# A selective-scan kernel: in the blocks behind a projection, the side chain runs one place later

## The chip, the cores and the metric

One core of a Trainium2 chip runs the whole program. The metric is the device time of one execution in microseconds (us), as the median of several runs. Smaller is better.

## The reference, cut to what matters

Sixteen images of 64 x 64 pixels and 96 channels go through two layers, each added to its input. Layer 0 normalises, upsamples with a Fourier interpolation, applies two 1 x 1 projections with a quadratic between them, and downsamples again. Layer 1 normalises, projects, convolves 3 x 3, and then runs a selective scan in four directions over the 4096 pixels. The scan is what fills the time:

```
delta = softplus(dts + dt_bias)
h = exp(dt * A) * h + (dt * u) * b
y = sum over the 16 states of h * c
```

`dts`, `b` and `c` are projections of the convolved rows `u`; there are 192 channels, 16 states and four directions. At the end the four results are added, normalised, gated and projected back to 96 channels.

## The kernel before, in words

**The scan.** The function `scan` (line 831) goes over 128 *steps*: each of the 16 images has 8, namely 4 forward and then 4 backward, and a step covers 1024 pixels. A step has six *blocks* (line 826), and a block four *units*. One unit (lines 1165 to 1249) covers two groups, "odd" and "even", of 128 partitions each:

- `decay` (L1039) is an exponential on ScalarE (ACT) into PSUM, one for each of the two groups. There is one PSUM buffer for each group, so the next decay waits until VectorE (DVE) is done with the last one.
- `drive` (L1045) is a product of 128 x 2048 on GpSimd (POOL). It is issued two units ahead.
- `recur` (L1054 forward, L1056 backward) is the scan itself, on DVE, first the odd group, then the even one.
- The read-out multiplies by `c`: on DVE for the even group (L1225); for the odd group on POOL (L1208) in units 0 to 2, and on DVE (L1215) in unit 3. `read_out` (L1079) then sums over the states with 16 small matmuls on TensorE (PE), eight a group.
- `keep` (L1062) copies the last state of a group, which the next step starts from.

**Places.** Every unit has three places, called with `slot(0)`, `slot(1)` and `slot(2)` (L1202, L1224, L1231): after the odd scan, after the even scan, and at the end behind the even read-out product, the next even decay and `read_out`. At each of them one step is taken of `all_work` (L916), the side chain, and after it perhaps one of the background (L1141). So a block has twelve places, p = 0 to 11; place p is place p mod 3 of unit p // 3. Every engine executes its own queue in the order in which the instructions were issued here.

**The side chain.** For each block one `task` (L878) makes 512 columns of `delta` (the softplus) and of the *step-size product* `dtu` that the next step needs. It starts with a matmul for `s` (L886), then ACT takes the *magnitude* m and e = exp(-m) (L893, L894), then w = 1 + e and the *logarithm* d (L897, L898), then ACT finishes w (L901) and PE adds *four sums* into `s` (L903), then DVE makes `dtu` from `s` (L907), ACT copies `delta` (L908), and both go to DRAM (L910, L911). In blocks 2 and 3 of a step the projection `pp` of the next step (L866) is issued at the last place, p = 11, and it uses the same PSUM buffer as `s`. So in the blocks behind a projection, blocks 3 and 4, the task is *late*: first ACT must empty `pp` with the copy `pr` (`mixed`, L871; its two writes of `rows` to DRAM go to a list that SyncE (SP) empties with the next units), and only then `s` may start. The late task has shorter pauses (the `late` counts at L891, L895, L899). Before the change these places are: copy 1, `s` 2, magnitude 4, logarithm 5, four sums 7, `dtu` 10, writes 11.

**The background.** While an image is scanned, `front` (L301) prepares the next one and `finish` (L591) ends the last one, a small piece at a time, mostly at the third place of a unit. In the fourth image's scan, steps 0 to 3 hold the quadratic layer, steps 4 and 5 the convolution (L556, with its two ACT_TABLE_LOADs around the Silu at L572 to L574), and the end of step 5 to step 7 the normalisation and output of the image before (L620 to L672). In `finish`, `rooted` (L641) makes a DVE product (L642) of the matmul `o_ps` (L697).

Of the kernel before, what the change touches and what calls it, by code (L numbers as in the profile page):

```python
# [78 lines left out]
def tile_two_blocks(  # L79
# [141 lines left out]
    def send(kept=0):  # L221
        while len(put_off) > kept:
            args, kwargs = put_off.pop(0)
            nc.sync.dma_start(*args, **kwargs)
# [606 lines left out]
    def scan():  # L831


        with ExitStack() as es:
# [13 lines left out]
            def open_step(st):  # L848
                ctxs[st].update(
                    rows=dctx.tile([2, 2 * NS, T], F32, name="rows"),  # L850
                    delta=[dctx.tile([128, T], F32, name=f"delta_d{v}") for v in range(3)],
                    dtu=[dctx.tile([128, T], F32, name=f"dtu_d{v}") for v in range(3)],
                    pr={},
                )

            def fetch_u(st, v, t):
                mi, _, lc = steps[st]
                uv = up_.tile([128, TB], F32, name="u")
                nc.sync.dma_start(out=uv, in_=image[mi]["xs"][v, :, lc * T + t:lc * T + t + TB])
                return uv  # L860

            def mix(st, us, ps):
                pair = steps[st][1]
                pp = ps.tile([128, TB], F32, name="pp", tag="g")
                for v in range(3):
                    nc.tensor.matmul(pp, lhsT=xpt_s[:, pair, v, :], rhs=us[v], start=(v == 0), stop=(v == 2))  # L866
                return pp

            def mixed(st, t, pp):
                pr = prp.tile([128, TB], F32, name="pr")  # L870
                nc.scalar.activation(pr, pp, AF.Identity, bias=bumps_s)  # L871
                for r in range(2):
                    later(
                        out=ctxs[st]["rows"][r, :, t:t + TB], in_=pr[64 * r:64 * r + 2 * NS, :]
                    )
                ctxs[st]["pr"][t] = pr

            def task(st, k, ps, make, late=False):  # L878

                v, t = tasks[k]
                ctx, pair = ctxs[st], steps[st][1]
                u = fetch_u(st, v, t)
                s = ps.tile([128, TB], F32, name="s", tag="g")
                nc.tensor.matmul(  # L886
                    s, lhsT=dtw_s[:, pair, v, :], rhs=ctx["pr"][t], start=True, stop=False, skip_group_check=True
                )
                yield
                e, d, m, w = (make(k) for k in ("e", "d", "m", "w"))  # L890
                for _ in range(1 if late else 2):  # L891
                    yield
                nc.scalar.activation(m, s, AF.Abs, scale=2.0)  # L893
                nc.scalar.activation(e, m, AF.Exp, scale=-1.0)  # L894
                for _ in range(1 if late else 2):  # L895
                    yield
                nc.scalar.activation(w, e, AF.Identity, bias=one_s)  # L897
                nc.scalar.activation(d, e, AF.Ln, bias=one_s)  # L898
                for _ in range(2 if late else 3):  # L899
                    yield  # L900
                nc.scalar.activation(w, w, AF.Identity, scale=-1.0, bias=one_s)  # L901
                for by, of in ((half_s, m), (ident_s, w), (ident_s, e), (ident_s, d)):
                    nc.tensor.matmul(s, lhsT=by, rhs=of, start=False, stop=(of is d), skip_group_check=True)  # L903
                for _ in range(3):
                    yield
                dtu, delta = make("dtu"), make("delta")
                nc.vector.tensor_mul(dtu, s, u)  # L907
                nc.scalar.copy(delta, s)  # L908
                yield
                nc.sync.dma_start(out=ctx["dtu"][v][:, t:t + TB], in_=dtu)  # L910
                nc.sync.dma_start(out=ctx["delta"][v][:, t:t + TB], in_=delta)  # L911
# [4 lines left out]
            def all_work(mi_of):  # L916

                chain = [(st + (k > 5), k % 6) for st in range(len(steps)) for k in (3, 4, 5, 6, 7, 8)]
                current = task(*chain[0], gps, near)
                next(current)  # L920
                pp = waiting = None
                for b in range(len(chain)):
                    mine, bi = divmod(b, len(blocks))
                    more = mine + 1 < len(steps)
                    for p in range(3 * NQ):
                        if pp is not None and p == 1:
                            mixed(*pp)
                            pp = None
                        elif p == 2 and waiting is not None:
                            current, waiting = waiting, None  # L930
                        if current is not None:
                            next(current, None)
                        if more and bi in (2, 3):
                            if p == 3:
                                if bi == 2:
                                    if steps[mine + 1][0] > mi_of():
                                        ahead_gen.drain()
                                        send()
                                    open_step(mine + 1)
                                us = [fetch_u(mine + 1, v, TB * (bi - 2)) for v in range(3)]  # L940
                            elif p == 11:
                                pp = mine + 1, TB * (bi - 2), mix(mine + 1, us, gps)
                        if p == 11:
                            current = None
                            if b + 1 < len(chain) and chain[b + 1][0] < len(steps):
                                if pp is not None:
                                    waiting = task(*chain[b + 1], gps, near, True)
                                else:
                                    current = task(*chain[b + 1], gps, near)
                                    next(current)  # L950
                        yield
# [195 lines left out]

            last = len(units) - 1
            work = all_work(lambda: mi)
            for n in range(2):  # L1150
                drive(n)
# [13 lines left out]
            for n, (st, bi, j) in enumerate(units):  # L1165
# [71 lines left out]
                if j == 1 and n + 3 <= last and steps[units[n + 3][0]][1] == 1:  # L1237
                    st2, bi2, _ = units[n + 3]
# [124 lines left out]
```

## Time and profile before

| what | value |
|---|---|
| median of 3 runs | 20050.83 us (20045.97 to 20051.76) |
| the profiled execution | 20052.4 us |
| its span, first to last instruction | 20050.6 us |
| granted TensorE clock, mean | 0.876 |
| ACT busy | 13339.3 us (67%) |
| PE busy | 16526.3 us (82%) |
| DVE waits for ACT `da`, L1056 and L1054 | 135.8 + 99.7 + 30.7 + 7.4 us |
| ACT waits for PE before the copy `pr` L871 | 251.1 us, 134 times |
| ACT waits for PE before the magnitude L893 | 223.6 us, 124 times |
| DVE waits for PE before `dtu` L907 | 198.4 us, 57 times (the longest, 149.9 us, before the scan starts) |

An engine that is busy for most of the span need not be the bound at a given place: idle time counts where the engine that sets the pace stands still. The profile names, for each idle stretch, what released the engine. A line of the timeline reads: start, duration, engine, source line, operation, result <- inputs, shape, count, and in brackets the idle time before it.

### The profile page before, as it was taken

Reading aid. Unit: us, or ns where it says so; the run is one execution under the profiler, and the core shown is the slowest. Engines: PE = TensorE matmul, PEld = TensorE weight load, DVE = VectorE, ACT = ScalarE, POOL = GpSimd, SP = SyncE. Lnnn points to the kernel's source line nnn. Section 1 sums busy time; section 2 is a strip of 40 time slices with the busy share of each in tenths; the row PEclk is TensorE's granted clock in tenths of the full one; section 3 lists DMA queues with packets and bytes.
Section 4 is the critical chain, followed back from the end, with each engine's and each line's share of the span. In section 5 each row is a group of like instructions: output and inputs, shape, how many; then the busy total and the mean of one; then the engine's idle time right before and its main releaser. Section 6 shows DMA issues by size and latency. Waiting matters only on the chain. (4 is left out here: it accounts for less than half of the span.)

```text
span 20050.6 us, 275225 instructions
## 1 busy us (share of the span) xinstructions
PE 16526.3 (82%) x98604; PEld 7189.9 (36%) x98604; DVE 19133.1 (95%) x13040; ACT 13339.3 (67%) x19798; POOL 19176.4 (96%) x5403
## 2 busy tenths in 40 slices
PE   7877888888888888888888888888888888887965
PEld 4423334333343433334333343333434334343321
DVE  1999999999999999999999999999999999999999
ACT  4666766667666676767667666676666766666654
POOL 1999999999999999999999999999999999999999
PEclk8887898988889888898988889889898888989977
DMA  3666676766667666676766767667676676767755
GB/s 90 218 232 208 231 236 217 242 220 231 231 221 239 218 231 235 221 243 215 235 229 222 242 211 242 221 223 242 212 249 213 231 237 218 246 209 238 247 209 186
DMA packets 1979481, 4481.77 MB, mean 224 GB/s; under 512 B 465022, under 2 KB 564254, under 8 KB 1976190
## 3 DMA queue, kind: packets, MB, share of 16 engines
q1 hardware_dynamic: 1978110, 4464.15, 65.4%
q8 instruction: 779, 12.76, 0.3%
q14 instruction: 592, 4.85, 0.1%
HBM read 3585.05 MB, written 878.18 MB: 223 GB/s over the span
## 5 line engine op out<-in xcount | busy, mean ns | idle before, releaser
L1045 POOL TENSOR_TENSOR b<-dtu,bt 128x2048 f32<-128x2048 f32 x3072 | 13913.0, 4541 | 527.6 <-DMA dtu<-dtu_d 464.4
L1039 ACT ACTIVATE da<-delta,a_s 128x1024 f32<-128x1024 f32 x6144 | 6850.4, 1115 | 2264.7 <-DVE b L1225 799.1
L1208 POOL TENSOR_TENSOR odd<-b,ct 128x1024 f32<-128x1024 f32 x2304 | 5445.3, 2363 | 296.1 <-DVE b L1056 196.2
L1079 PE MATMUL y<-b,fold_s 128*32 128x256 f32 x30720 | 2642.5, 439 | 2559.4 <-DVE b L1225 2534.7
L1225 DVE TENSOR_TENSOR b<-da,ct 128x1024 f32<-128x1024 f32 x3072 | 3748.3, 1220 | 13.6
L1056 DVE TENSOR_TENSOR_SCAN da<-da,new,b 128x1024 f32<-128x1024 f32 x1440 | 3337.8, 2336 | 113.0 <-ACT da L1039 100.2
L1054 DVE TENSOR_TENSOR_SCAN da<-da,new,b 128x1024 f32<-128x1024 f32 x1440 | 3339.1, 2337 | 31.6 <-ACT da L1039 16.2
L1062 ACT COPY new<-da 128x1 f32<-128x1 f32 x2880 | 453.4, 157 | 3345.1 <-DVE b L1225 1842.5
L1079 PEld LDWEIGHTS y<-b,fold_s 128*32 128x32 f32 x30720 | 744.1, 116 | 4729.1 <-DVE b L1225 2708.6
L1056 DVE TENSOR_TENSOR_SCAN b<-da,new,b 128x1024 f32<-128x1024 f32 x864 | 2020.9, 2339 | 52.0 <-ACT da L1039 51.6
L1054 DVE TENSOR_TENSOR_SCAN b<-da,new,b 128x1024 f32<-128x1024 f32 x864 | 2022.5, 2341 | 0.1
L1079 PE MATMUL y<-odd,fold_s 128*32 128x256 f32 x18432 | 1609.6, 423 | 121.5 <-POOL odd L1208 116.1
L556 PE MATMUL c_ps<-xgp,wtap_s 96*64 96x512 f32 (+1 forms) x4608 | 1645.2, 609 | 5.5 <-ACT xgp L523 5.5
L422 PE MATMUL h_ps<-wide,w1t_s 96*128 96x500 f32 x1920 | 1114.6, 693 | 178.7 <-ACT wide L429 102.0
L449 PE MATMUL o_ps<-w2c_s,wide 128*100 128x96 f32 x9600 | 1071.8, 277 | 87.5 <-ACT wide L429 85.6
L449 PEld LDWEIGHTS o_ps<-w2c_s,wide 128*100 128x100 f32 x9600 | 1031.4, 191 | 277.9 <-ACT wide L429 155.8
L1056 DVE TENSOR_TENSOR_SCAN da<-da,b 128x1024 f32<-128x1024 f32 x480 | 1085.5, 2280 | 41.1 <-ACT da L1039 35.6
L1054 DVE TENSOR_TENSOR_SCAN da<-da,b 128x1024 f32<-128x1024 f32 x480 | 1084.0, 2277 | 39.1 <-POOL b L1045 24.7
L903 PE MATMUL s<-m,half_s 128*128 128x512 f32 x1534 | 1071.3, 787 | 1.0 <-ACT m L893 1.0
L886 PE MATMUL s<-pr,dtw_s 128*128 128x512 f32 x1536 | 1068.1, 784 | 0.0
L903 PE MATMUL s<-w,ident_s 128*128 128x512 f32 x1534 | 947.6, 704 | 141.8 <-ACT w L901 139.3
L556 PEld LDWEIGHTS c_ps<-xgp,wtap_s 96*64 96x64 f32 (+1 forms) x4608 | 593.1, 168 | 939.1 <-issue 904.7
(179 smaller groups left out, 21896.6 us busy)
## 6 DMA issues: line engine op xcount, KB each, us to landing
dtu<-dtu_d SPq DMA_DIRECT2D x1536, 512.0 KB
delta<-delta_d SPq DMA_DIRECT2D x1536, 512.0 KB
bt<-rows SPq DMA_DIRECT2D x1024, 512.0 KB
ct<-rows SPq DMA_DIRECT2D x1024, 512.0 KB
u<-xs_d SPq DMA_DIRECT2D x1544, 256.0 KB
dtu_d<-dtu SPq DMA_DIRECT2D x767, 256.0 KB
delta_d<-delta SPq DMA_DIRECT2D x767, 256.0 KB
wide<-in_x SPq DMA_DIRECT2D x768, 128.0 KB
```

The source lines that it names most:

```text
L422: nc.tensor.matmul(h_ps[j], lhsT=w1t_s[:, 128 * j:128 * (j + 1)], rhs=xu.rearrange("c p q -> c (p q)"), start=True, stop=True,)
L449: nc.tensor.matmul(o_ps[:, p, :], lhsT=hsq[j][:, UPS * p:UPS * (p + 1)], rhs=w2c_s[:, j, :], start=(j == 0), stop=(j == HB - 1),)
L556: nc.tensor.matmul(c_ps[p:p + n], lhsT=wtap_s[:, tap, 128 * i:128 * i + n], rhs=xgp[:, h0:h0 + 8, dx:dx + HW], start=(tap == 0), stop=(tap ...
L886: nc.tensor.matmul(s, lhsT=dtw_s[:, pair, v, :], rhs=ctx["pr"][t], start=True, stop=False, skip_group_check=True)
L903: nc.tensor.matmul(s, lhsT=by, rhs=of, start=False, stop=(of is d), skip_group_check=True)
L1039: nc.scalar.activation(da, deltas[n // NQ, e], AF.Exp, scale=a_s[:, k, g, units[n][2]:units[n][2] + 1])
L1045: nc.gpsimd.tensor_mul(b, dtus[n // NQ], bt.unsqueeze(1).to_broadcast([128, 2, T]))
L1054: nc.vector.tensor_tensor_scan(out, da, b, before, ALU.mult, ALU.add)
L1056: nc.vector.tensor_tensor_scan(out[:, ::-1], da[:, ::-1], b[:, ::-1], before, ALU.mult, ALU.add)
L1079: nc.tensor.matmul(y[32 * q:32 * q + 32, e, :], lhsT=fold_s, rhs=weighed[e][:, QT * q:QT * q + QT], start=(pair == 0 and j == 0 and e == 0 ...
L1208: nc.gpsimd.tensor_mul(odds[n], h, bc[1, r, j])
L1225: nc.vector.tensor_mul(bs[n][:, 0, :], h, bc[1, r, j])
```

## The change

`late` tasks get everything up to the four sums one place later, and one pause less between the sums and `dtu`. The late places become: copy 2, `s` 3, magnitude 5, logarithm 6, four sums 8, `dtu` 10, writes 11. Blocks that are not behind a projection, and the order on DVE and POOL, stay as they were. The `rows` writes of a late copy are handed to SP one unit later.

```
@@ task
                 for by, of in ((half_s, m), (ident_s, w), (ident_s, e), (ident_s, d)):
                     nc.tensor.matmul(s, lhsT=by, rhs=of, start=False, stop=(of is d), skip_group_check=True)
-                for _ in range(3):
+                for _ in range(2 if late else 3):
                     yield
                 dtu, delta = make("dtu"), make("delta")
@@ all_work
                     for p in range(3 * NQ):
-                        if pp is not None and p == 1:
+                        if pp is not None and p == 2:
                             mixed(*pp)
                             pp = None
-                        elif p == 2 and waiting is not None:
+                        elif p == 3 and waiting is not None:
                             current, waiting = waiting, None
```

More of the change, by code (lines that the diff above doesn't have):

```diff
@@ L903, in task @@
                     nc.tensor.matmul(s, lhsT=by, rhs=of, start=False, stop=(of is d), skip_group_check=True)
-                for _ in range(3):
+                for _ in range(2 if late else 3):
                     yield
@@ L925, in all_work @@
                     for p in range(3 * NQ):
-                        if pp is not None and p == 1:
+                        if pp is not None and p == 2:
                             mixed(*pp)
                             pp = None
-                        elif p == 2 and waiting is not None:
+                        elif p == 3 and waiting is not None:
                             current, waiting = waiting, None
```

## The prediction

> **What bounds the kernel.** I read the page's first part, then the stages of one image (the fourth) as windows, then what POOL and DVE waited for, then the timeline of single blocks.
>
> ```profile
> PE 16526.3 (82%) x98604; PEld 7189.9 (36%) x98604; DVE 19133.1 (95%) x13040; ACT 13339.3 (67%) x19798; POOL 19176.4 (96%) x5403
> ```
>
> Two engines look full. The windows (length, then busy time of PE, PEld, DVE, ACT, POOL) tell them apart; these are steps 2, 4, 5 and 6:
>
> ```profile
> 4393.94:4542.80 148.86, 132.00 (x1121) 74.70 (x1122) 148.07 (x103) 104.04 (x165) 148.86 (x43) 0.83 0.65 223
> 4691.91:4843.76 151.85, 119.10 (x668) 42.59 (x668) 145.98 (x108) 115.19 (x180) 149.40 (x43) 0.90 0.68 236
> 4843.76:4995.07 151.31, 126.67 (x588) 50.41 (x588) 148.47 (x103) 110.79 (x153) 150.82 (x43) 0.92 0.72 242
> 4995.07:5156.35 161.28, 137.94 (x600) 48.49 (x600) 152.71 (x112) 100.20 (x146) 150.88 (x43) 0.91 0.77 257
> ```
>
> In step 2 POOL never rests: 148.86 us is POOL's own work, 24.8 us a block. A step costs more only where POOL waits: about 3 us more in steps 4 and 5, 12 in step 6 (and 11 in step 7, 2.6 in step 1). So a DVE stall costs only what it makes POOL wait.
>
> How much DVE may be late follows from POOL's queue. The last unit of a block has no odd product, so behind the product for a block's first unit POOL has a whole further product (4.55) before the odd one that needs DVE's odd scan (2.34). DVE may start a block 4.55 - 2.34 = 2.2 us after its product is ready; I call this the **lag**. Beyond 2.2 (2.1 in the rows) POOL stands still. DVE wins back about 0.25 a block, 0.75 in steps 0 and 4. In step 4 the lag is 1.24 at block 3 and 2.81 at block 4 (4795.39 against a product that ended 4792.58), and there POOL waits 0.7. In steps 0, 2 and 3 it stays under 1.5 at blocks 3 to 5: a cover of 0.6 to 1.5 us.
>
> Why block 3 of step 4 loses time:
>
> ```profile
> 4777.42 2.30 DVE L1056 TENSOR_TENSOR_SCAN da<-da,b 128x1024 f32<-128x1024 f32 x1 [0.62 <-ACT da L1039]
> 4784.69 2.30 DVE L1056 TENSOR_TENSOR_SCAN da<-da,b 128x1024 f32<-128x1024 f32 x1 [1.51 <-ACT da L1039]
> ```
>
> ```profile
> 4775.50 0.69 ACT L871 ACTIVATE pr<-pp,bumps_s 128x512 f32<-128x512 f32 x1 [2.63 <-PE pp L866]
> 4782.20 0.60 ACT L893 ACTIVATE m<-s 128x512 f32<-128x512 f32 x1 [3.77 <-PE s L886]
> ```
>
> ```profile
> 4781.03 1.12 PE L886 MATMUL s<-pr,dtw_s 128*128 128x512 f32 x2
> 4782.09 3.66 PE L556 MATMUL c_ps<-xgp,wtap_s 96*64 96x512 f32 x16
> ```
>
> ACT stands in front of the copy and of the magnitude, with the decay that DVE needs queued behind each. These are the 0.62 and the 1.51 us. PE has no gap from 4775.39 to 4793.24: it is behind, not waiting.
>
> **The change, part by part.**
>
> *The copy, one place later.* It now stands behind the next even decay. The wait for `pp` still comes, but what is queued behind it is an odd decay with 2.3 us to spare. Gain: 0.62 in step 4, the same 0.64 in block 3 of step 5.
>
> *`s` and the magnitude.* `s` moves from the end of unit 0 to place 0 of unit 1, so on PE it is now queued behind the background that is issued in between. In the convolution that is the 3.66 us row above. The magnitude moves behind the even decay, so its deadline relaxes: behind it stands the odd decay for unit 3, which DVE needs only at the end of unit 2, one unit (5.7) after the end of unit 1. Taking off m and e (1.25) and the decay (1.12), `s` may end 3.3 us behind the end of unit 1; before it was 0.3 us ahead of it. So 3.6 us of room are won and up to 3.66 lost, and it is the block that decides.
> Step 4, block 3: `s` ends at 4782.15 + 3.6 = 4785.8, the decay at 4788.2. DVE, freed of 2.13, ends unit 2 at 4788.25 - 2.13 = 4786.1: a stall of 2.1. The logarithm's two rows (1.3) now follow this decay, so the next one ends at 4790.8, 0.4 late. The finish of w (0.70) then stands ahead of the Silu chain, which took 3.77 (4789.61 to 4793.37) and had 0.40 to spare; it ends near 4795.3, and the decay of the next block is 0.85 late. Sum 3.35 for 2.13: **+1.2**.
> Step 5, block 3, in the same way (stalls 0.64 + 1.05; `s` ends 4931.78 + 3.53): 1.45 + 0.25 + 0.8 for 1.69: **+0.8**.
> Their block 4 had a small or no stall; `s` there keeps its deadline by 0.3, and only the Silu chain is later: 0 to 1.0, I take **+0.3** each. Lag is already at its limit in both steps, so all this reaches POOL.
>
> *The four sums.* They move behind `read_out` of unit 2, which needs DVE's even product and POOL's odd one. In steps 0 to 3 POOL's odd product ends up to 2.3 us after DVE's, so the sums end near 2.3 + 0.6 + 3.7 = 6.6 us after unit 3's scan could start, where `dtu` is due after 5.6: a new stall of about 1.0 less the lag. It cures itself, because it raises the lag; at the limit it would be 1.0 on a cover of 0.6 to 1.5. I take 0. Without that cover it costs 1.0 for each of 8 blocks an image.
> In step 6 there is no cover, and something stands behind the sums:
>
> ```profile
> 5093.10 1.12 PE L903 MATMUL s<-m,half_s 128*128 128x512 f32 x2
> 5097.74 2.12 PE L697 MATMUL o_ps<-yz,ow_s 128*96 128x512 f32 x4
> ```
>
> ```profile
> 5101.14 0.67 DVE L642 TENSOR_TENSOR wide<-o_ps,wide 96x512 f32<-96x512 f32 x1
> ```
>
> Now PE idles until the even product ends (5093.79 + 1.20 = 5094.99), reads out (1.07) to 5096.05, then does the sums (3.7, and up to 0.3 for w) to 5100.0, then `o_ps` to 5102.1. DVE asks for it at 5101.2: **+0.9**. Block 4 of step 6 is PE-bound and ends nearly the same; step 7 wins 0.8 in block 3 (its `o_ps` is no longer behind `s`) and loses about as much in the later `dtu`; together I take **+0.3**.
>
> *Gains elsewhere.* Block 4 of step 1 loses 0.63 to the copy's wait with the lag at 2.34; half of it reaches POOL: **-0.3**. Its block 3 has a `dtu` stall of 1.6 that stays (its sums stand behind other matmuls either way), between -0.7 and +1.0.
>
> *SP and DMA.* The task's fetch of `u` goes out 2.3 us later and is used seven places later. The `rows` writes leave one unit later; block 4's are read back at its unit 3, still two units (12 us) on. I take 0; if that cover went, POOL would wait for `bt`, where its longest wait is now 3.1 us. POOL and DVE queues keep their order.
>
> The clock: half-rate windows are in the rows. The read-out's 16 matmuls took 1.93 us at 4769.02 against 1.07 at 4795.53. The Trainium skill, "TensorE: Matmul & The Clock Gate", section "What's actually happening", says that PE falls to half rate after an idle window of about 3.4 us and needs as long a busy one to come back. This speaks against the change, as PE now waits ahead of the sums; by the rule the new gaps (up to 2.3 us) alone are too short, so the sum stays, and if they were enough, 3.7 us of sums would become 7.4. Without the rule: sums as long as 6.1 us are in the trace (4336.02 to 4342.14), 2.4 over the usual, which is my upper end for a late block.
>
> **The sum.** 1.2 + 0.8 + 0.3 + 0.3 + 0.9 + 0.3 - 0.3 = 3.5 us an image. The convolution of a next image and the finish of a last one each run beside 15 of the 16 images: +52 us. Against the profiled execution, 20052.4, which is 1.6 over the median of the runs, this gives 20,104; for the median I say **20,103**.
>
> **Rivals.**
> 1. *Faster: the stalls go and none comes back.* It decides at one point, whether `s` ends within 3.3 us of the end of unit 1 in the convolution. For it: the deadline relaxes by 3.6, and everywhere but there the moved `s` has time. Against: the 3.66 us of c_ps in a PE queue without a gap. Price: POOL's waits at blocks 4 and 5 go, 0.7 in step 4, 0.5 in step 5, 0.75 in step 1, and about 1 in step 7: 2.9 x 15 = 44. Time 20,007.
> 2. *Nothing to see.* Gains and losses balance, or lag hides both: 20,050. For it: steps 0 to 3 have cover, and the stalls of steps 4 and 5 largely only change their place.
> 3. *Much slower.* The read-out's wait stops the sums in every late block, at half clock too, and the cover of steps 0 to 3 is used up: 1.0 x 8 x 15 = 120 on top: 20,223. Against: the lag cures it.
> That the queues are not moved as told is no rival: in the changed program `s` stands behind c_ps, and the sums behind the read-out.
>
> **How the numbers follow.** Forecast 0.50, rival 1 0.13, rival 2 0.30, rival 3 0.07. About 0.2% (40 us) is what a measurement of this kernel can tell from no change. The forecast's own terms run from +20 to +95 us, so 0.08 of its 0.50 lies within 0.2%. Faster 0.13, same 0.38, slower 0.49. The range takes in rival 1 and most of the way to rival 3: 20,005 to 20,185.
>
> **What would show it.** Right: in steps 4 and 5, block 3, the bracket before the even scans of units 1 and 2 is gone and one of 1 to 2.5 us stands before the odd scan of unit 3; `o_ps` L642 waits near 1 us in step 6; `dtu` L907 waits more than its 198 us in all; POOL's waits for DVE grow by some 50 us. Wrong: no stall before unit 3's odd scan (rival 1), or windows of steps 2 and 3 well over 149 us (rival 3).

## The result, and the profile after

| | before | after |
|---|---|---|
| median (4 runs each) | 20048.4 us (20034.6 to 20051.8) | 20236.6 us (20231.6 to 20257.1) |
| the profiled execution | 20052.4 us | 20257.1 us |
| its span | 20050.6 us | 20255.3 us |
| granted TensorE clock | 0.876 | 0.872 |

The changed kernel is slower: ratio 1.0097, 95% interval 1.0085 to 1.0109, or 188 us where 52 were forecast and 20,185 was the upper end of the range. The profiled execution of after is the longest of its four; the traces differ by 204.7 us. Rival 3 (20,223) came nearest.

The first part of the page, for after: the engines do the same work in a longer span.

```profile
PE 16575.1 (82%) x98604; PEld 7170.8 (35%) x98604; DVE 19133.6 (94%) x13040; ACT 13339.5 (66%) x19798; POOL 19176.9 (95%) x5403
```

So the difference is idle time of POOL. POOL's waits in before, then in after (what it waited for: us in total, times, longest):

```profile
POOL odd L1208 <- DVE b L1056: 196.2, 167, 3.5
POOL b L1045 <- DMA bt<-rows: 47.7, 24, 3.1
...
POOL odd L1208 <- DVE b L1054: 24.5, 46, 2.5
```

```profile
POOL odd L1208 <- DVE b L1056: 266.6, 163, 5.9
POOL odd L1208 <- DVE b L1054: 139.1, 99, 2.8
POOL b L1045 <- DMA bt<-rows: 62.7, 28, 3.9
```

The two rows in which POOL waits for DVE's odd scan grew from 220.7 to 405.7 us: 185 of the 205 us. L1054 is the forward scan, so most of it lies in steps 0 to 3. DVE's own waits in after say what it stood at:

```profile
DVE dtu L907 <- PE s L903: 458.3, 204, 150.4
...
DVE da L1056 <- ACT da L1039: 104.5, 56, 5.5
DVE b L1056 <- ACT da L1039: 90.8, 72, 5.7
...
DVE yz L638 <- ACT sq L633: 28.8, 16, 2.0
```

`dtu` waits 458 us for the four sums; before it was 198. DVE's waits for the decay (ACT `da`) fell from 274 us to 202; in run 1 below, which has the same copy and `s` without the sums' move, they are 241, so only half of that fall is the gain of the copy. The fourth image's steps 0, 2 and 6 as windows:

```profile
4141.35:4293.98 152.63, 111.86 (x781) 50.06 (x782) 145.66 (x105) 105.67 (x184) 147.20 (x43) 0.74 0.64 214
4444.16:4595.14 150.98, 131.24 (x1122) 73.78 (x1122) 148.10 (x103) 103.67 (x165) 149.32 (x43) 0.84 0.63 216
5049.21:5215.50 166.29, 140.28 (x600) 48.67 (x600) 152.79 (x111) 99.74 (x146) 150.74 (x43) 0.90 0.75 249
```

Step 2 had been all POOL at 148.86; now POOL rests 1.7 us in it. Step 0 went from 147.74 to 152.63, step 6 from 161.28 to 166.29, and steps 4 and 5, where the prediction saw the main loss, hardly moved (151.02 and 151.76, before 151.85 and 151.31). One image is one sample; below, "a step lost" means the mean over images 2 to 15 of the distance between the first odd scans of two steps, less the same in before:

| us an image, by step | 0 | 1 | 2 | 3 | 4 | 5 | 6 | 7 | sum |
|---|---|---|---|---|---|---|---|---|---|
| after | +3.9 | -0.6 | +2.7 | +2.0 | -0.4 | +0.5 | +3.4 | -0.4 | +11.0 |

These 14 images make 153 of the 204.7 us; image 1 took 18.9 longer, the last image with the end 25.8, and 6.6 came before the scan. Each such row is one profiled execution. The four runs of after lie 25 us apart, 1.6 us an image, so a difference of a few tenths between rows says nothing.

The timeline shows what happens in a late block. In step 0, block 3, of the fourth image, first PE, then DVE:

```profile
4232.47 1.08 PE L1079 MATMUL y<-b,fold_s 128*32 128x256 f32 x8 [0.55 <-DVE b L1225]
4234.35 1.08 PE L1079 MATMUL y<-odd,fold_s 128*32 128x256 f32 x8 [0.80 <-POOL odd L1208]
4235.36 2.08 PE L903 MATMUL s<-m,half_s 128*128 128x512 f32 x2
4237.23 1.90 PE L903 MATMUL s<-w,ident_s 128*128 128x512 f32 x2
4238.94 1.05 PE L903 MATMUL s<-e,ident_s 128*128 128x512 f32 x2
4239.83 1.02 PE L903 MATMUL s<-d,ident_s 128*128 128x512 f32 x2
```

```profile
4232.34 4.47 DVE L1054 TENSOR_TENSOR_SCAN da<-da,b 128x1024 f32<-128x1024 f32 x2
4236.71 1.20 DVE L1215 TENSOR_TENSOR b<-da,ct 128x1024 f32<-128x1024 f32 x1
4240.89 0.69 DVE L907 TENSOR_TENSOR dtu<-s,u 128x512 f32<-128x512 f32 x1 [2.97 <-PE s L903]
```

Unit 3's scans start at 4232.34. PE must first read out unit 2, whose odd half waits for POOL's product; the sums start 3.0 us behind unit 3's start and take 5.5 us, as matmuls that take 1.0 us elsewhere take 1.9 and 2.1. DVE is ready for `dtu` at 4237.92 and gets it at 4240.89. The next block starts late by this, and there POOL stands still for DVE's first odd scan:

```profile
4245.05 2.35 POOL L1208 TENSOR_TENSOR odd<-b,ct 128x1024 f32<-128x1024 f32 x1 [1.80 <-DVE b L1054]
```

In before, in the same block, unit 3's scans start at 4185.50. The sums were on PE ahead of the read-out, were nearly as slow (5.0 us), and ended before DVE asked for `dtu`:

```profile
4184.74 2.07 PE L903 MATMUL s<-m,half_s 128*128 128x512 f32 x2
...
4188.69 1.02 PE L903 MATMUL s<-d,ident_s 128*128 128x512 f32 x2
4189.64 0.64 PE L1079 MATMUL y<-b,fold_s 128*32 128x256 f32 x8
```

```profile
4191.01 0.68 DVE L907 TENSOR_TENSOR dtu<-s,u 128x512 f32<-128x512 f32 x1
```

### The profile page after: what moved, and what is told of

Same layout as the page of the kernel before. It is cut to its first block, busy times and chain, and to the rows that moved or that the text cites. A ratio compares the mean times of both kernels' runs of the same rounds, so it can differ in the third digit from the quotient of the medians.

```text
span 20255.3 us, 275626 instructions
## 1 busy us (share of the span) xinstructions
PE 16575.1 (82%) x98604; PEld 7170.8 (35%) x98604; DVE 19133.6 (94%) x13040; ACT 13339.5 (66%) x19798; POOL 19176.9 (95%) x5403
## 5 line engine op out<-in xcount | busy, mean ns | idle before, releaser
L1054 DVE TENSOR_TENSOR_SCAN da<-da,new,b 128x1024 f32<-128x1024 f32 x1440 | 3338.1, 2337 | 1.1 <-ACT new L1062 0.5
L1054 DVE TENSOR_TENSOR_SCAN b<-da,new,b 128x1024 f32<-128x1024 f32 x864 | 2022.8, 2341 | 0.2
L903 PE MATMUL s<-w,ident_s 128*128 128x512 f32 x1534 | 993.8, 735 | 142.9 <-ACT w L901 137.4
L1054 DVE TENSOR_TENSOR_SCAN da<-da,b 128x1024 f32<-128x1024 f32 x480 | 1083.6, 2276 | 12.7 <-POOL b L1045 12.6
L886 PE MATMUL s<-pr,dtw_s 128*128 128x512 f32 x1536 | 1019.7, 751 | 15.5 <-ACT pr L871 15.4
L907 DVE TENSOR_TENSOR dtu<-s,u 128x512 f32<-128x512 f32 x767 | 522.7, 682 | 462.1 <-PE s L903 458.3
```

The lines of the kernel that those rows point to most:

```text
L886: nc.tensor.matmul(s, lhsT=dtw_s[:, pair, v, :], rhs=ctx["pr"][t], start=True, stop=False, skip_group_check=True)
L1054: nc.vector.tensor_tensor_scan(out, da, b, before, ALU.mult, ALU.add)
```

## The experiments

Three theories stood at the start. **A**: the place of the four sums, behind the read-out of unit 2 and so behind POOL's odd product, is the whole loss, through DVE's wait at `dtu`. **B**: the later copy and the later `s`, behind the background, are. **C**: the half clock is, since PE now pauses ahead of the sums. Times are medians; beside them before took 20046.9 us (runs 1 to 4), 20048.1 (5 to 8), 20038.4 (9 to 11) and 20051.0 (12), and the ratios are to these.

**1. Only the sums back.** Late places: copy 2, `s` 3, magnitude 5, logarithm 6, sums 7, `dtu` 10. Edit against after:

```
@@ task, the pauses ahead of the sums
-                for _ in range(2 if late else 3):
+                for _ in range(1 if late else 3):
@@ task, the pauses ahead of dtu
-                for _ in range(2 if late else 3):
+                for _ in range(3):
```

> Copy, s, magnitude and logarithm at the later places of the change (2, 3, 5, 6), the four sums back at place 7, ahead of the read-out of unit 2. Theory A (the sums' place behind that read-out is the whole cost): the time is back within 60 us of before, 19,990 to 20,090, and the wait of dtu L907 for PE is back near 200 us. Rival B (the later copy and the later s, behind the background's matmuls, are the cost): 20,180 or more, with the waits of the scans for the decay as in the changed kernel.

Measured: 20060.0 us, ratio 1.0006 [0.9997, 1.0015]; `dtu` waits 193.3 us. Without the sums' move the loss is gone.

**2. Only the sums later.** Before, with the sums at 8 and `dtu` at 10, the rest as it was.

```
@@ task, the pauses ahead of the sums
-                for _ in range(2 if late else 3):
+                for _ in range(3):
@@ task, the pauses ahead of dtu
-                for _ in range(3):
+                for _ in range(2 if late else 3):
```

> The kernel before with the four sums alone one place later (copy 1, s 2, magnitude 4, logarithm 5, sums 8, dtu 10). Theory A: 20,190 to 20,280, dtu L907 waits 400 us or more, as in the changed kernel. Rival B: within 60 us of before, near 20,050.

Measured: 20259.2 us, ratio 1.0104 [1.0089, 1.0119]; `dtu` waits 482.5 us. The sums' move alone makes all of the loss. Theory B falls as the cause.

**3. The clock held up.** After, with two more `s` matmuls at place 7 of late blocks, which write the same values again and keep PE busy.

```
@@ task, the pauses ahead of the sums
-                for _ in range(2 if late else 3):
+                for i in range(2 if late else 3):
                     yield
+                    if late and i == 0:
+                        for _ in range(2):
+                            nc.tensor.matmul(
+                                s, lhsT=dtw_s[:, pair, v, :], rhs=ctx["pr"][t], start=True, stop=False, skip_group_check=True
+                            )
```

> The changed kernel with two more matmuls of s from the same operands (the same value, written again) at place 7 of the late blocks, so that PE is busy while it waits ahead of the read-out. Rival C (the half clock in the four sums is the cost): the sums run at full clock, 3.7 us, the wait of dtu falls by 1 us a block in steps 0, 2 and 3, the time falls to 20,150 or less. Theory A (the sums start too late whatever the clock): 20,200 to 20,300, since the read-out waits for POOL's odd product as before and PE has 1.9 us more to do in each late block.

Measured: 20241.1 us, ratio 1.0097 [1.0082, 1.0112]. All but 15 of the 254 late sums took the 3.70 us of the full clock, and steps 0 and 3 lost only 0.4 and 0.3 us, but steps 1, 4 and 7 now lost 1.8, 2.9 and 3.0. There the wait at `dtu` grew (in block 3 from 1.8, 0.1 and 0.3 us to 3.1, 1.2 and 2.1), presumably because the added matmuls stand in PE's way. The total had been expected at 20,150 or less by C and above 20,200 by A; but since the edit brings work of its own, the total doesn't settle C. Run 12 does.

**4. The odd half of the read-out behind the sums.** After, but in unit 2 of blocks 3 and 4 the eight matmuls on POOL's product are issued behind place 8.

```
@@ read_out
                 for e in range(2):
+                    if e == 1 and j == 2 and bi in (3, 4):
+                        yield
@@ the unit, around slot(2)
-                read_out(n)
+                reading = read_out(n)
+                next(reading, 0)
...
+                next(reading, 0)
```

> The changed kernel, but in unit 2 of blocks 3 and 4 the odd half of the read-out is issued behind place 8, so that the four sums wait for DVE's even product alone and not for POOL's odd one. Theory A, in the form that POOL's odd product is what the sums wait for: the wait of dtu falls by 1.5 to 2 us a block, and the time to 20,060 to 20,130. If it is the matmuls ahead of them on PE and not the wait for POOL: no change, 20,200 to 20,260.

Measured: 20088.4 us, ratio 1.0020 [1.0010, 1.0030]; `dtu` waits 255.8 us. Nearly four fifths of the loss (148 of 188 us) hung on the odd half, its wait for POOL's product and its own 1 us, ahead of the sums. Of what is left, 2.4 us an image, step 6 makes +3.4, and the other steps together -1.0.

**5 and 6. The copy's gain, and `s` beside it.** Run 5 has `s` directly behind the copy at place 2, magnitude 5, logarithm 6, sums 7; against after:

```
-                        elif p == 3 and waiting is not None:
+                        if p == 2 and waiting is not None:
```

with the pauses that put the rest at those places. Run 6 is before with the copy alone moved to place 2 (`s` 2, magnitude 4, logarithm 5, sums 7).

> Late places: copy 2, s 2 (directly behind the copy, so no longer behind the background of the next place), magnitude 5, logarithm 6, sums 7, dtu 10. Theory A (only the place of the four sums behind the read-out of unit 2 costs time): the loss is gone as in the run with the sums at 7; 20,020 to 20,060; DVE's wait for dtu near 195 us as before, DVE's waits for the decay below the 136 us of before in L1056. If the convolution in front of s (the prediction's 1.2 + 0.8 us for steps 4 and 5) costs anything, steps 4 and 5 are here 1 to 2 us an image shorter than in the run with the sums at 7. Rival B (the later copy and magnitude cost): 20,100 or more.

> Before, with the late copy moved from place 1 to place 2 alone (s 2, magnitude 4, logarithm 5, sums 7, dtu 10 as before). The prediction's step for the copy: 0.6 us less before the even scan in block 3 of steps 4 and 5 and 0.3 in block 4 of step 1, so at most 1.5 x 15 = 23 us faster: 20,024 to 20,050. If ACT is merely late a place further, the magnitude waits longer (above 224 us in all) and the time is as before, 20,047, within 15.

Measured: 20005.4 us, ratio 0.9978 [0.9970, 0.9987], and 20008.5 us, ratio 0.9980 [0.9971, 0.9989]. Both beat both kernels, by more than was expected. In run 5, steps 4 and 5 together are 3.9 us an image shorter than in run 1, so `s` behind the convolution does cost that. Block 3 of step 4, DVE in run 5: of the stalls of 0.62 and 1.51 us before the even scans none is left, and one of 0.85 stands at `dtu`.

```profile
4775.69 2.27 DVE L1056 TENSOR_TENSOR_SCAN da<-da,b 128x1024 f32<-128x1024 f32 x1
...
4779.14 4.47 DVE L1056 TENSOR_TENSOR_SCAN da<-da,b 128x1024 f32<-128x1024 f32 x2
4783.52 1.20 DVE L1215 TENSOR_TENSOR b<-da,ct 128x1024 f32<-128x1024 f32 x1
4785.57 0.69 DVE L907 TENSOR_TENSOR dtu<-s,u 128x512 f32<-128x512 f32 x1 [0.85 <-PE s L903]
```

**7. `dtu` later too.** After, with `dtu`, the delta copy and their writes at place 11.

```
@@ task, the pauses ahead of dtu
-                for _ in range(2 if late else 3):
+                for _ in range(3):
@@ task, the pause ahead of the two writes
-                yield
+                if not late:
+                    yield
```

> As changed, and dtu, the delta copy and their two writes at place 11 in late blocks. Theory A (the distance from sums to dtu is what costs: DVE stands at dtu because the sums end up to 2 us late): DVE's wait for dtu falls from 458 us to 150 to 260; the time lies near 20,090, within 40 (step 6 keeps its 3 us an image). Rival D (the wait at dtu is only where a late PE shows, and the sums behind the read-out cost PE or ACT time however late dtu is): the wait moves to pp or to another matmul's reader, and the time stays above 20,180.

Measured: 20222.6 us, ratio 1.0088 [1.0072, 1.0103]. Theory A had 20,090 and missed. The wait at `dtu` fell to 316.2 us, not to 260, because one place is only one product of 1.2 us, and PE got a wait that after does not have:

```profile
PE pp L866 <- ACT delta L908: 75.8, 69, 1.9
```

The projection of block 3 uses the buffer of `s` and now stands behind the delta copy. Step 4 loses 3.3 us an image here where after gains 0.4. The two effects were not separated by a run.

**8. No wait for the sums, first try.** After, with late `dtu` made of m:

```
-                nc.vector.tensor_mul(dtu, s, u)
+                nc.vector.tensor_mul(dtu, m if late else s, u)
```

> As changed, but in late blocks dtu is made of m instead of s, so that DVE waits for no sums there; everything else, PE's order and the delta copy too, is as changed. Its step-size product in late blocks is another number than the reference's. Theory A: the loss but for step 6 is gone, with the 1.6 us of step 1 that before has as well: 20,060, within 40; step 6 stays about 3 us an image longer than before, through o_ps and the square that stand behind the sums. Rival D: above 20,180.

Measured: 20901.9 us, ratio 1.0425 [1.0411, 1.0439]: neither theory. The groups of line 907 (duration min/median/max in ns) show that the edit did more than it said:

```profile
L907 DVE TENSOR_TENSOR dtu<-s,u x513: 665/678/693, 430.5 to 20751.6; 128x512 f32<-128x512 f32 x171
L907 DVE TENSOR_TENSOR dtu<-m,u x254: 973/4980/6253, 548.5 to 20648.7; 128x512 f32<-128x512 f32 x127
```

m lies in SBUF where s lay in PSUM, and the product takes 4.2 us in the mean instead of 0.68; 254 x 3.55 = 902 us, more than the whole loss. The last section comes back to it. For the theories the run is void.

**9. No wait for the sums, second try.** After, with late `dtu` made at place 7 of s as it stands before the sums, in PSUM.

```
@@ task, the pauses ahead of the sums
-                for _ in range(2 if late else 3):
+                for i in range(2 if late else 3):
+                    if late and i == 1:
+                        dtu = make("dtu")
+                        nc.vector.tensor_mul(dtu, s, u)
```

> As changed, but in late blocks DVE makes dtu at place 7 from s as it is before the four sums, one operand in PSUM as before, so DVE waits for no sums. Its step-size product in late blocks leaves the sums out; PE's and ACT's work and their order are as changed, the delta copy still waits for the sums. Theory A (DVE's wait for the sums is the cost): DVE's wait for dtu falls to about 150 us, and the time to 20,090 or less, with step 6 alone still 2 to 3 us an image over before. Rival D (late sums cost in PE or ACT also without DVE's wait): 20,180 or more.

Measured: 20135.7 us, ratio 1.0050 [1.0033, 1.0066], between the two. `dtu` waits 179.1 us. Step by step: steps 0 to 5 and 7 together are 0.4 us an image below before, where after has lost 7.6; so in sum what they lost went through DVE's wait. Single steps are less clean: steps 2 and 3 still lose 1.2 and 1.4, and step 1 wins 1.9, part of it the wait at `dtu` that before has there too. Step 6 alone loses 5.1. In its block 3 DVE stands at the next reader behind the sums. The run has waits of its own besides: the early `dtu` waits 32.0 us for m, 14.9 for u and 6.3 for d, and 1.19 of it in the block shown, ahead of the even product. So the 5.1 isn't all the sums'. DVE, then PE, in step 6, block 3:

```profile
5127.75 0.69 DVE L642 TENSOR_TENSOR wide<-o_ps,wide 96x512 f32<-96x512 f32 x1 [2.52 <-PE o_ps L697]
```

```profile
5119.67 1.08 PE L1084 MATMUL y<-b,fold_s 128*32 128x256 f32 x8 [4.07 <-DVE b L1230]
5120.52 1.08 PE L1084 MATMUL y<-odd,fold_s 128*32 128x256 f32 x8
5121.53 1.65 PE L906 MATMUL s<-m,half_s 128*128 128x512 f32 x2
...
5125.60 2.05 PE L697 MATMUL o_ps<-yz,ow_s 128*96 128x512 f32 x4
```

PE idles 4 us for the even product, then reads out, then sums, and only then makes `o_ps`.

**10. The fourth corner.** After with `s` at place 2 (sums at 8).

```
-                        elif p == 3 and waiting is not None:
+                        if p == 2 and waiting is not None:
```

with one pause more ahead of the magnitude.

> Late places: copy 2, s 2, magnitude 5, logarithm 6, sums 8, dtu 10: as changed, but s directly behind the copy. With the runs that have sums at 7 (s at 2: 20,005; s at 3: 20,060) this fills the square of two moves. If the moves add: 20,237 - 55 = 20,182, within 25, with steps 4 and 5 together 3 to 4 us an image shorter than as changed. If the late sums hide the late s: as changed, 20,237, within 20.

Measured: 20212.2 us, ratio 1.0087 [1.0072, 1.0102]; 174 over its own before (interval 144 to 204), where adding gave 135. By these medians the moves don't add: `s` at 3 costs some 55 us with the sums at 7, and some 14 with the sums at 8, a difference that lies within the two intervals. The steps say otherwise: an image gains 2.8 us by `s` at 2 with the sums at 7 and 2.6 with the sums at 8. Whether the moves add stays open. Where the gain falls did change: steps 4 and 5 won 1.2 us, not 3 to 4, and step 6 won 2.1.

**11. Three sums before the read-out, one behind it.** After, with m, e and d added at place 7 and w, now last (in the other blocks too), at 8.

```
-                for by, of in ((half_s, m), (ident_s, w), (ident_s, e), (ident_s, d)):
+                for by, of in ((half_s, m), (ident_s, e), (ident_s, d), (ident_s, w)):
+                    if late and of is w:
+                        yield
```

> As changed (copy 2, s 3, magnitude 5, logarithm 6), but the sums of m, e and d at place 7 and only that of w, now the last, at place 8; dtu 10. Behind the read-out of unit 2 stands one matmul pair of about 1.0 us instead of 3.7. Theory A (the length of what stands behind that read-out): the last sum ends 2.7 us earlier, the stalls of up to 2.9 before dtu all but go, 20,060 as with all sums at 7, within 30. If any wait behind the read-out costs, whatever its length: over 20,150.

Measured: 20060.7 us, ratio 1.0009 [1.0000, 1.0019], on the spot. PE in step 0, block 3, of the fourth image:

```profile
4182.13 1.02 PE L905 MATMUL s<-d,ident_s 128*128 128x512 f32 x2
4183.08 0.64 PE L1081 MATMUL y<-b,fold_s 128*32 128x256 f32 x8
4183.54 0.61 PE L1081 MATMUL y<-odd,fold_s 128*32 128x256 f32 x8
4184.08 1.13 PE L905 MATMUL s<-w,ident_s 128*128 128x512 f32 x2
```

The last sum stands behind the same read-out, but nothing else does: it ends at 4185.2, and DVE asks for it at 4186.7. Step 6 loses nothing either (-0.4). What counts is how long the work is that stands behind the read-out; the three other sums run while its products are still being made. In this run ACT also finishes w at place 7, one place earlier than in after; run 4, which leaves w where after has it, bears the reading without that.

**12. The clock held up in steps 0 and 3 alone.** Run 3, with the fill in those steps only:

```
+                    if late and i == 0 and (st - 1) % 8 in (0, 3):
```

> As changed, with the two re-issued s matmuls at place 7 of the late blocks in steps 0 and 3 of each image alone, where filling all late blocks had taken 3.5 and 1.8 us an image off the loss. Half clock as the price of those two steps: step 0 falls to about 0.4 and step 3 to about 0.3 us over before, every other step stays as changed, and the time falls by 5.2 x 16 = 83 to 20,155, within 25. If the loss only moves on to the next steps (the fall in steps 0 and 3 was paid by steps 1, 4 and 7 even without fill there): 20,237, within 20.

Measured: 20182.2 us, ratio 1.0065 [1.0048, 1.0081]; steps 0 and 3 lose 0.3 and 0.1 us, as expected; steps 1, 2 and 6 are 0.8, 0.4 and 0.4 us longer than in after, so a part is paid back, and the time misses the 20,155 by 27 us. The wait at `dtu` fell by 71 us, the time by 54. The half clock is thus a real price where it falls on the sums, in these two steps 54 of the 188 us; it is no cause of its own, since with the sums at place 7 it costs nothing that shows. In before the late sums of steps 0 to 3 were as slow (4.6 us in the mean, 4.7 in after).

All runs beside one another, in us an image by step:

| places | time, us | 0 | 1 | 2 | 3 | 4 | 5 | 6 | 7 |
|---|---|---|---|---|---|---|---|---|---|
| before (copy 1, `s` 2, sums 7) | 20047 | 0 | 0 | 0 | 0 | 0 | 0 | 0 | 0 |
| 2: copy 1, `s` 2, sums 8 | 20259 | +3.9 | -0.1 | +4.1 | +1.2 | -1.0 | +1.1 | +2.0 | +0.4 |
| 6: copy 2 alone | 20009 | -0.1 | -1.4 | +1.2 | -0.6 | -1.6 | -1.0 | +0.3 | -0.2 |
| 5: copy 2, `s` 2, sums 7 | 20005 | 0.0 | -1.4 | +0.9 | -0.4 | -1.9 | -1.6 | +0.6 | +1.0 |
| 1: `s` 3, sums 7 | 20060 | +0.2 | -2.0 | +1.3 | -0.6 | +0.7 | -0.4 | +1.2 | -0.5 |
| 11: `s` 3, last sum 8 | 20061 | +0.1 | +0.1 | +0.5 | -0.4 | +0.4 | +1.5 | -0.4 | -0.6 |
| 10: `s` 2, sums 8 | 20212 | +3.9 | -0.5 | +3.3 | +2.0 | -1.6 | +0.5 | +1.3 | -0.5 |
| after: `s` 3, sums 8 | 20237 | +3.9 | -0.6 | +2.7 | +2.0 | -0.4 | +0.5 | +3.4 | -0.4 |

So the change is three moves: the copy gains some 40 us, `s` behind the background gives these back, and the sums behind the read-out cost 175 on top of the two (212 by themselves, run 2).

## Why the prediction was wrong, by its own steps

*What bounds the kernel* held: POOL sets the pace, a DVE stall costs what it makes POOL wait, and 185 of 205 us are in the rows where POOL waits for DVE.

*The four sums* is the step that failed: "It cures itself ... I take 0." Its start was right: the sums were put near 2.9 us behind unit 3's start, and 3.0 is in the timeline (2.2 to 3.1 in the means of the late blocks of steps 0 to 3). Two things were wrong. The sums' length was taken as 3.7 us and was 5.35 in the mean in both late blocks of step 0, 5.2 in block 4 of step 2, 5.0 and 4.7 in step 3; the 6.1 us row was in hand, but kept for the upper end only. And the cure was counted on.

The cover itself was read well: in step 0, block 3, the lag at unit 3 was 0.35 us (the scans start at 4232.34, their product ended at 4231.99), and without the stall the next block would have started with a lag of 0.9, which is 1.2 under the limit of 2.1. But the stall was 2.97, so that block starts 3.85 us late (at 4242.63, its product ended at 4238.78), 1.75 over the limit, and POOL stands still. Nor does the raised lag last until the next stall, which falls in unit 3: there it is 0.86 again, and only so much comes off. In the mean the two stalls of step 0 are 2.89 and 2.34 us, and its late blocks lose 2.2 and 2.0. With sums of 3.70 us (run 12) the stalls in step 0 are 1.0 and 0.65 and the step loses 0.3: for that length the cure was rightly argued. Steps 0 to 3 lost 7.9 us an image, 119 us over 15. That rival 3 had priced this at 120 is in part luck: it put 1.0 on each of the eight late blocks, and they lost from nothing (step 1) to 2.2.

*Steps 4 and 5* were forecast at +1.2, +0.8 and twice +0.3, 2.6 in all, and came to +0.1. Of this their late blocks lost 0.4, 0.4, -0.3 and 1.1, together 1.6, and block 0, which the forecast left alone, won 1.2 and 0.3; why it did is not shown. The 1.1 is block 4 of step 5 and not the Silu chain that the forecast had there: `dtu` waits 1.55 us, for sums of 5.25 us. In block 3 of step 4 the mechanism is there. ACT in step 4, block 3, and DVE there:

```profile
4828.97 0.67 ACT L871 ACTIVATE pr<-pp,bumps_s 128x512 f32<-128x512 f32 x1
...
4838.16 0.60 ACT L893 ACTIVATE m<-s 128x512 f32<-128x512 f32 x1 [3.48 <-PE s L886]
```

```profile
4840.53 4.68 DVE L1056 TENSOR_TENSOR_SCAN da<-da,b 128x1024 f32<-128x1024 f32 x2 [1.55 <-ACT da L1039]
...
4848.73 2.29 DVE L1056 TENSOR_TENSOR_SCAN b<-da,b 128x1024 f32<-128x1024 f32 x1 [0.45 <-ACT da L1039]
```

The copy no longer waits, and the stall stands before unit 3's odd scan, as foretold: 1.55 for 2.1. The two smaller stalls added behind it (0.4 and 0.85) came to 0.45 in one place. Runs 5 and 1 give the gross sizes of the two blocks 3 with the sums at 7: 3.5 us won by the later copy and magnitude (1.5 by the copy alone, run 6), and 4.2 lost by the later `s`; the forecast had 3.8 (2.13 + 1.69) and 5.85.

*Step 6*: `o_ps` (+0.9) was right in kind. L642 waits 1.07 us in block 3 in the mean, 0.07 before; with the `dtu` stall (0.64) that block lost 1.7. It loses as much with the sums' move alone (run 2), and 0.1 with the sums at 7 (run 1): the sums' place carries it. That block 4 would end "nearly the same" was wrong: it lost 1.5, at the later square (`yz` L638, waits there 1.95 us, 0.16 before). This is not the sums' doing: with the sums at 7 and `s` at 3 it is still 1.1 (run 1), and with `s` at 2 it is 0.4, though the sums are at 8 (runs 2 and 10). So it comes with the later `s`. (In run 11 the wait at the square is 1.44, but there the 1.16 us at L642 that before has in this block are gone.) *Step 7* took -0.4, for the +0.3 that it shared with block 4 of step 6. *Step 1* gained 0.6, for 0.3; the copy alone gains 1.4 there (run 6). *SP and DMA* at 0: POOL's wait for `bt` rose by 15 us in the profiled pair; in runs 1 to 12 it lies 5 to 13 us over before, in run 2 too (7), which leaves the copy where it was, so that the later writes are its cause is not shown.

*The clock.* The page's rule on an idle window was applied, and it gave no price; the next section shows what the trace has in its place. *The chances*: slower was the likeliest sign, but rival 3, given 0.07, should have weighed as much as the forecast, since the row of 6.1 us was enough to use the cover up.

## What to carry to other kernels

When work is moved behind another instruction of an in-order queue, add up the start by the wait ahead of it and the *slowest* length that it has in that stage, and hold the stall that comes of it against the slack that is left. Slack that each block gives back cannot be counted on twice: look at its value in the very unit where the next stall falls. If a sum of several pieces must cross a late point, keep all pieces but one ahead of it (run 11), and if a change is made of several moves, run them singly: here one gained 40 us and another lost 175 or more.

## What the runs showed of the hardware

**Half clock without a long pause.** In after, step 0, block 3, the windows around the sums (length, then busy time of PE, PEld, DVE, ACT, POOL, then the granted clock):

```profile
4228.74:4232.16 3.42, 2.07 (x26) 1.25 (x26) 3.42 (x4) 3.38 (x6) 3.42 (x2) 1.00 0.99 376
4232.16:4235.58 3.42, 2.31 (x17) 0.62 (x18) 3.42 (x3) 3.35 (x6) 3.42 (x2) 0.50 0.06 24
4235.58:4238.99 3.41, 3.41 (x5) 1.34 (x6) 2.34 (x2) 1.00 (x2) 3.41 (x2) 0.50 0.02 5
```

The clock is halved at 4232.16 after a window in which PE was busy 2.07 of 3.42 us, with no pause over 1.1 us; it stays so for 6.8 us although PE is full in the second half. The Trainium skill, "TensorE: Matmul & The Clock Gate", section "What's actually happening", puts the half rate behind at least one idle window of about 3.4 us. This trace has it behind a window that was six tenths busy, and the measurement decides: the prediction's "too short" does not follow. The whole trace of after, cut into the stretches of 3.41 us at whose ends the clock changes, says more (PE busy as the profile has it). At full clock all 386 stretches with PE busy for under 40% were followed by half clock, of those with 40 to 60% 244 of 446, and of those with more 35 of 3541. At half clock none of the 574 stretches under 80% was followed by full clock; of the 943 above, 665 were. Before gives the same picture (464 of 464, 182 of 342, 37 of 3574; none of 469, 683 of 982). The stretch shown above is thus one of the rare ones; but where PE was busy for under four tenths of a stretch, the clock was halved every time.

**A product of two SBUF operands on DVE waits for POOL.** In run 8 all 254 products of m and u end 0.55 us behind the end of one of POOL's products (0.547 to 0.555), however early they start. With s in PSUM the same product took 0.68 us beside the same POOL work. The Trainium skill, "SBUF — State Buffer", section "SBUF: two separate sides", calls the port pair that DVE and GpSimd share an exclusive lock, held for a whole instruction, and names two SBUF inputs on DVE as one of its cases; run 8 agrees, and its price here was 3.6 us for each product.
